# Transposing normalised tokens: TensorE against VectorE squares and a trip through DRAM

## The chip, the cores and the metric

The kernel runs on one core of a Trainium2 chip. A core has TensorE (PE, with its weight loads shown as PEld), VectorE (DVE), ScalarE (ACT), GpSimd (POOL), and the queue engine SyncE (SP), which here only issues DMAs. The metric is device time in microseconds of one execution; the number that counts is the median of several runs.

## The reference

The model is one sandwich layer on x of shape 16 x 256 x 256 (sequences, tokens, width E = 256), all in float32:

```
x = x + layernorm(attention(layernorm(x)))
x = x + layernorm(ffn(layernorm(x)))
```

Attention has 16 heads of 128: q = x Wq^T; shared keys and values kp, vp of width 128, each multiplied per head by a factor kh, vh that comes from a gated, decayed running sum over tokens (weights Wkvh, Wg); rotary embedding on q and k; causal softmax; output through Wout. The FFN has 1024 hidden units with ternary-quantised weights: silu(gate) * up, an RMS norm, and a projection back to 256.

Both products after a layernorm (the projections of attention, and gate and up of the FFN) contract over E. The normalised tokens come with tokens on partitions, and TensorE needs E on partitions, so each normalised sequence (256 x 256) has to be transposed. This transposition is what the change is about.

## The kernel before

The 16 sequences go in 8 pairs (`BP = 2`, a pair has 512 tokens). Each pair has 16 heads, so there are 128 heads in a row, and the main loop has one *slot* for each: `slot(g)` scores head g, softmaxes it, turns the probabilities of head g-1, and forms the output of head g-2. In front of that it prepares the queries of head g+1 and the keys of head g+2. Slot numbers are given below modulo 16, so that "slot 0" is the first head of a pair; the slot is then the same one in each pair.

The order of the instructions on each engine is the order in which the program writes them (`manual_schedule`); no planner moves them. Everything that isn't a head's own work is put into named places of slots: `put(slot, place, step)` appends a step to a plan, and `slot(g)` runs the places in the order first, scored, turned, emptied, projection, last as its own work goes by (in the code below, `fill(g, place)`; the place names come in this order: "first" at the slot's start, "scored" after the next queries' matmuls, "turned" after `queries_done`, then `reciprocals`, "projection", `outputs` of head g-2, "emptied", "last"). Each engine runs its own instructions in order and waits by semaphores for the others.

A slot's own work, by engine:

- PE: scores `sps` (L575), queries `qps` (L285), whatever projection `att` (L735) is planned, head output `ops` (L691, L698).
- DVE: `prob` (L588: mask, scale, row minimum), the head's turn `sq` (L634), the rotary embedding of the next head's queries (L307 twice, L315, and L318, which writes `qT`), and the reciprocals `total` (L609). The next slot's `sps` needs `qT`.
- ACT: `even` (L627: probabilities divided and laid out for the turn), `prob` (L598: exponentials), the copy `oT` (L706).
- POOL: `kT` (L563) and `vph` (L675).
- SP: fetches the key factors `kh` (L545, for four heads ahead), writes the turned probabilities to DRAM (`moved`, L641) and reads them back (`pT`, four reads, L647).

That turn of probabilities (`Head.turn`) already works as the change does: VectorE transposes each 32 x 32 square in place, and the DMAs move the squares to where they belong by way of DRAM. `even` of 128 x 768 takes one DVE instruction, one write and four reads.

The normalised tokens go another way. In `Pair.plan` (attention, pair bp, planned during the pair before) and `After.plan` (FFN, sequence q) a sequence goes through these steps:

- `moments`: DVE statistics (L232 twice, L234 twice);
- `normalise`: POOL takes the inverse root and applies mean and scale, xn (L219, L221, L261; DVE for the first pair);
- `transpose`: four TensorE transposes of 128 x 128 into a PSUM tile (`transposed`, L278, tp_a or tp_f);
- attention: `keep`, an ACT copy into `xnT` (L349). From `xnT` come `hg` (`factors`, gates and head factors), `kp` (`keys`), `vps` (`values`), and all `qps` of the pair;
- FFN: `split` into a high and a low float32r part, `xhi` on ACT (L780) and `xlo` on DVE (L781), from which `gates` and `ups` are multiplied.

For pairs 2 to 7 the attention steps stand in slots 14 to 1 (`s = end - H - 2`, so moments in 14 and 15, transposes in 0 and 1), `hg` in slot 2 "last" and the rotary embedding of the shared keys in slot 5 (`rope.sine` "scored", `keys_done` "emptied"). The FFN of the even sequence of the pair before has its statistics in slot 6 and its transposes and split in slot 8; the odd one has its statistics in slot 0 and transposes and split in slot 2. All of PE's results in the ordinary path go through four PSUM tiles (`ps_mm`, tag "mm"), and the tokens through two buffers `xn`, the turned probabilities through two buffers `sq32`.

Of the kernel before, what the change touches and what calls it, by code (L numbers as in the profile page):

```python
# [9 lines left out]
F32 = mybir.dt.float32  # L10
# [6 lines left out]
P = 128  # L17
B, N, E = 16, 256, 256
# [5 lines left out]
BP = 2  # L24
T = BP * N
NT = T // P
EC = E // P
# [13 lines left out]
def sandwich_kernel(  # L41
# [13 lines left out]
    nc = tc.nc  # L55
# [3 lines left out]
    p2 = ctx.enter_context(tc.tile_pool(name="p2", bufs=2))  # L59
    p3 = ctx.enter_context(tc.tile_pool(name="p3", bufs=3))  # L60
    heads = ctx.enter_context(tc.tile_pool(name="heads", bufs=10))
    dram = ctx.enter_context(tc.tile_pool(name="dram", bufs=2, space=bass.MemoryType.DRAM))
# [36 lines left out]
    for half in range(2):  # L99
        cols = slice(half * H * D // 2, (half + 1) * H * D // 2)  # L100
        nc.scalar.dma_start(
            out=wq_sb[:, :, cols], in_=wq[:, cols].rearrange("(c p) f -> p c f", p=P)
# [120 lines left out]
    class Rows:  # L223
# [35 lines left out]
        def apply(self, dst, src, engine):  # L259
            for t in range(self.count):  # L260
# [6 lines left out]
                    ALU.mult,  # L267
                )

    def tiles(ap):  # L270
        return [ap[:, t, :] for t in range(2)]

    def transposed(xn, name):

        tp = mm_tile([P, EC, N], f"tp_{name}")
        for c in range(EC):
            for t in range(2):
                nc.tensor.transpose(  # L278
                    tp[:, c, t * P : (t + 1) * P], xn[:, t, c * P : (c + 1) * P], ident
                )  # L280
        return tp
# [42 lines left out]
    def put(slot, place, *steps):  # L324
        assert place in PLACES
        plan.setdefault((slot, place), []).extend(steps)


    class Pair:
# [12 lines left out]

        def transpose(self, b):
            self.tp[b] = transposed(self.xn[b], f"a{self.bp}_{b}")

        def keep(self, b):
            if b == 0:
# [144 lines left out]
        def plan(self):  # L492

            end = self.bp * H
            s = end - H - (2 if self.bp > 1 else -1)
            for b in range(BP):
                put(s + b, "scored", lambda b=b: self.moments(b))
                put(s + b, "emptied", lambda b=b: self.normalise(b))
                put(s + 2 + b, "turned", lambda b=b: self.transpose(b))
                put(s + 2 + b, "emptied", lambda b=b: self.keep(b))  # L500
            put(s + 4, "last", self.factors)
            put(s + 5, "first", self.gates)
            put(s + 5, "scored", self.raw_factors)
            put(s + 5, "last", self.keys)
            put(s + 7, "scored", lambda: self.rope.sine(0), lambda: self.rope.sine(1))
            put(s + 7, "emptied", self.keys_done)
            chain = end - (7 if self.bp > 1 else 8)
            put(chain - 2, "emptied", self.sigmoids)
            put(chain - 1, "emptied", self.decays)
            put(chain, "scored", self.decayed)  # L510
            put(chain + 1, "scored", self.sums)
            put(chain + 2, "first", self.rows_out)
            put(chain + 3, "last", self.value_factors)
            put(chain + 4, "first", self.value_factors_done)
            put(end - 1, "last", self.values)
            put(end, "first", self.values_done)
# [194 lines left out]
    class After:  # L711
# [60 lines left out]
        def transpose(self):  # L772
            self.tp = transposed(self.xn, f"f{self.q}")

        def split(self):
            self.parts = [
                self.buffer([P, EC, N], F32R, f"x{k}", f"x{k}", p2)
                for k in ("hi", "lo")
            ]
            nc.scalar.copy(self.parts[0], self.tp)  # L780
            nc.vector.tensor_sub(self.parts[1], self.tp, self.parts[0].bitcast(F32))  # L781
# [224 lines left out]

        def plan(self, s):

            put(s, "scored", self.moments)
            put(s, "emptied", self.normalise)  # L1010
            put(s + 2, "turned", self.transpose)
            put(s + 2, "emptied", self.split)
            if self.late:
                return
            for u in range(FC // 2):
                at = s + 3 + (u + 1) // 2
                put(at, "last" if u % 2 == 0 else "scored", lambda u=u: self.gates(u))
                done = (at + 1, "first") if u % 2 == 0 else (at, "turned")
                put(*done, lambda u=u: self.gates_done(u))
            put(s + 6, "scored", self.silu)  # L1020
            for u in range(FC // 2):
                put(s + 7 + u, "first", lambda u=u: self.hidden(u))
                put(s + 7 + u, "scored", lambda u=u: self.pieces(u))
                put(s + 7 + u, "emptied", lambda u=u: self.square(u))
                put(s + 8 + u, "last", lambda u=u: self.project(u))
            for u in range(FC // 2):
                put(s + 6 + u, "last", lambda u=u: self.ups(u))
            put(s + 12, "first", self.last_moments)
            put(s + 11, "scored", self.fold)
            put(s + 12, "turned", self.sums)  # L1030
            put(s + 12, "emptied", self.sums_done)
            put(s + 13, "scored", self.inverse_roots, self.last_factors)
            put(s + 14, "first", self.finish)
            put(s + 14, "scored", self.store)
# [53 lines left out]
    for pair in all_pairs[1:]:  # L1088
        pair.plan()
        for b in range(BP):  # L1090
            q = pair.bp * BP + b
# [263 lines left out]
```

## Time and profile before

| | us |
|---|---|
| runs: median (lowest to highest of 3) | 1117.67 (1114.88 to 1118.01) |
| the profiled execution, its own time | 1118.2 |
| its span, first to last instruction | 1116.4 |
| one pair, from one slot 13 to the next (633.39 to 764.03) | 130.64 |

In the trace each slot begins with PE's first `sps`. The pair that the prediction reads has these starts (us): slot 0 at 526.10, 1 at 535.29, 2 at 542.75, 3 at 551.61, 4 at 558.72, 5 at 565.47, 6 at 575.33, 7 at 582.46, 8 at 589.58, 9 at 598.00. The pairs 2 to 6 repeat this to a few hundredths of a microsecond but for some slots. Slots 115 and 117, which the prediction speaks of as well, are slots 3 and 5 of the last pair and begin at 940.25 and 954.61.

How to read the lines. The line with the engines' busy times gives busy us, share of the span, and the number of records. In the table by stretches, each row has the stretch, its length, then for PE, PEld, DVE, ACT and POOL the busy us and the records, the granted TensorE clock (1.00 is full), the busy share of the DMA engines, and GB/s. A wait line has the waiting engine and instruction, what it waited for, and total us, times, and the longest. A timeline line has start and duration in us, engine, source line, operation, output<-inputs, shapes and count, and in brackets the idle time of the engine just before it and what ended that. Matmuls overlap and their ends are modelled, so the distance from one start to the next says what an operation holds PE for. SPq lines are the DMA issues.

### The profile page before, as it was taken

Reading aid. Unit: us, or ns where it says so; the run is one execution under the profiler, and the core shown is the slowest. Engines: PE = TensorE matmul, PEld = TensorE weight load, DVE = VectorE, ACT = ScalarE, POOL = GpSimd, SP = SyncE. Lnnn points to the kernel's source line nnn. Section 1 sums busy time; section 2 is a strip of 40 time slices with the busy share of each in tenths; the row PEclk is TensorE's granted clock in tenths of the full one; section 3 lists DMA queues with packets and bytes.
Section 4 is the critical chain, followed back from the end, with each engine's and each line's share of the span. In section 5 each row is a group of like instructions: output and inputs, shape, how many; then the busy total and the mean of one; then the engine's idle time right before and its main releaser. Section 6 shows DMA issues by size and latency. Waiting matters only on the chain.

```text
span 1116.4 us, 18641 instructions
## 1 busy us (share of the span) xinstructions
PE 1073.3 (96%) x5738; PEld 862.4 (77%) x5738; DVE 845.7 (76%) x2303; ACT 740.8 (66%) x2152; POOL 684.1 (61%) x757
## 2 busy tenths in 40 slices
PE   8899998999999999999999999999999999999986
PEld 5577775788778787888778887788878887788786
DVE  5878889867796777968788677877779677776365
ACT  2778766675676757767576766857567675767563
POOL 3767796438656585548665586555855465656343
PEclk9999999999999999999999999999999999999997
DMA  4512224444444444445454454444444444443101
GB/s 151 163 48 69 76 81 152 152 144 141 141 133 126 147 136 141 134 126 157 126 146 131 125 153 135 146 125 152 139 136 138 126 136 137 139 126 109 39 1 38
DMA packets 108611, 137.35 MB, mean 123 GB/s; under 512 B 12192, under 2 KB 76192, under 8 KB 108512
## 3 DMA queue, kind: packets, MB, share of 16 engines
q1 hardware_dynamic: 103344, 125.09, 36.7%
q0 software_dynamic: 2000, 6.56, 1.8%
q10 hardware_dynamic: 3168, 4.52, 1.2%
q8 instruction: 46, 0.75, 0.3%
q14 instruction: 53, 0.43, 0.1%
HBM read 88.41 MB, written 47.71 MB: 122 GB/s over the span
## 4 chain that ended last, share of the span: by engine, by line
PE 73%; DVE 14%; POOL 5%; ACT 5%; issue 2%; DMA 1%; SPq 0%; ACTq 0%; POOLq 0%; DVEq 0%
PE att L735 16%; PE qps L285 14%; PE sps L575 11%; PE ops L691 8%; PE ffn L882 6%; PE ups L789 5%; PE ops L698 4%; PE gps L789 3%; DVE turned_q L307 3%; ACT even L627 2%; DVE sq L634 2%; DVE qps L315 1%; DVE qT L318 1%; PE hg L285 1%; PE vps L285 1%
## 5 line engine op out<-in xcount | busy, mean ns | idle before, releaser
L598 ACT ACTIVATE prob<-prob,low 128x128 f32<-128x128 f32 (+1 forms) x512 | 225.8, 443 | 38.0 <-DVE low L588 37.6
L285 PE MATMUL qps<-xnT,wq_sb 128*128 128x512 f32 x512 | 240.8, 593 | 0.1
L735 PE MATMUL att<-wout_sb,oT 128*128 128x256 f32 x1024 | 239.1, 380 | 0.7 <-ACT oT L706 0.7
L735 PEld LDWEIGHTS att<-wout_sb,oT 128*128 128x128 f32 x1024 | 189.5, 190 | 40.5 <-issue 16.5
L706 ACT COPY oT<-ops 128x512 f32<-128x512 f32 x128 | 74.9, 585 | 217.8 <-PE ops L698 217.6
L588 DVE CUSTOM_DVE_ANT_0 prob<-sps,mask 128x128 f32<-128x128 f32 (+1 forms) x512 | 157.7, 352 | 79.2 <-PE sps L575 78.3
L575 PE MATMUL sps<-kT,qT 128*128 128x128 f32 (+1 forms) x1024 | 193.4, 332 | 18.3 <-DVE qT L318 10.7
L307 DVE TENSOR_TENSOR turned_q<-qps,sin_sb 64x512 f32<-64x512 f32 x256 | 176.2, 688 | 16.7 <-PE qps L285 11.4
L675 POOL TENSOR_TENSOR vph<-vp,vh 128x512 f32<-128x512 f32 x110 | 115.8, 1053 | 99.6 <-PE ops L698 99.6
L575 PEld LDWEIGHTS sps<-kT,qT 128*128 128x128 f32 x1024 | 145.8, 191 | 38.8 <-DVE qT L318 14.3
L563 POOL TENSOR_TENSOR kT<-kh,kr 128x512 f32<-128x512 f32 x128 | 165.6, 1294 | 11.7 <-PE sps L575 9.3
L627 ACT ACTIVATE even<-prob,total 128x128 f32<-128x128 f32 (+1 forms) x440 | 163.9, 446 | 6.6 <-DVE total L609 6.4
L285 PEld LDWEIGHTS qps<-xnT,wq_sb 128*128 128x128 f32 x512 | 95.9, 190 | 67.5 <-issue 61.2
L691 PE MATMUL ops<-pT,vph 128*128 128x256 f32 x440 | 131.4, 380 | 2.5 <-DMA pT<-moved 1.8
L835 POOL TENSOR_TENSOR lo<-h,hi 128x512 fp32r<-128x512 f32 x54 | 68.6, 1271 | 90.6 <-ACT hi L833 90.6
L634 DVE STREAM_TRANSPOSE sq<-even 128x768 f32<-128x768 f32 x110 | 107.2, 974 | 17.5 <-ACT even L627 16.0
L598 ACT ACTIVATION_READ_ACCUMULATOR prob<-prob,low 128x1 f32 x512 | 96.5, 189 | 0.0
L315 DVE TENSOR_TENSOR qps<-qps,cos_sb 128x512 f32<-128x512 f32 x128 | 89.6, 700 | 4.7
L698 PEld LDWEIGHTS ops<-pT,vph 128*128 128x128 f32 x440 | 83.6, 190 | 11.4
L318 DVE TENSOR_TENSOR qT<-qps,turned_q 128x512 f32<-128x512 f32 x128 | 88.6, 692 | 4.4
L853 POOL TENSOR_TENSOR squares<-squares,sq 128x512 f32<-128x512 f32 x39 | 49.9, 1279 | 66.4 <-ACT sq L852 66.4
L691 PEld LDWEIGHTS ops<-pT,vph 128*128 128x128 f32 x440 | 74.4, 191 | 14.9 <-issue 7.2
(165 smaller groups left out, 1950.4 us busy)
## 6 DMA issues: line engine op xcount, KB each, us to landing
moved<-sq SPq DMA_DIRECT2D x110, 384.0 KB, 2.3
pT<-moved SPq DMA_DIRECT2D x440, 96.0 KB, 2.2
kh<-rows SPq DMA_DIRECT2D x126, 256.0 KB, 3.4
xt<-in_x_dram SPq DMA_DIRECT2D x16, 256.0 KB, 2.9
out_dram<-y POOLq DMA_DIRECT2D x13, 256.0 KB, 3.4
wq_sb<-in_wq_dram ACTq DMA_DIRECT2D x2, 1024.0 KB, 9.6
wout_sb<-in_wout_dram ACTq DMA_DIRECT2D x1, 2048.0 KB, 15.6
w_gu<-in_wgu_dram POOLq DMA_DIRECT2D x8, 256.0 KB, 3.4
```

The source lines that it names most:

```text
L285: nc.tensor.matmul(ps, lhs[:, c, :], rhs[:, c, :], start=(c == 0), stop=(c == EC - 1))
L307: self.engine.tensor_mul(by_sequence(self.turned[a : a + HALF, :]), by_sequence(self.src[b : b + HALF, :]), over_sequences(sin_sb[b : b + ...
L563: nc.gpsimd.tensor_mul(self.kT, self.kh, self.pair.kr)
L575: nc.tensor.matmul(sps[:, cols], self.qT[:, n0 + i * P : n0 + (i + 1) * P], self.kT[:, n0 : n0 + (i + 1) * P], start=True, stop=True,)
L588: nc.vector.tensor_tensor_reduce(out=prob[:, cols], in0=sps[:, cols], in1=mask[:, P - i * P :], scale=-SCALE, scalar=F32_MAX, op0=ALU.add, ...
L598: nc.scalar.activation(prob[:, cols], prob[:, cols], AF.Exp, bias=low[:, i : i + 1], scale=-1.0, accum_out=self.total[:, b * 2 + i : b * 2 ...
L627: nc.scalar.activation(dst, src, AF.Copy, scale=self.total[:, 2 * b + i : 2 * b + i + 1])
L634: nc.vector.transpose(turned.rearrange("p k u q -> p (k u q)"), self.even.rearrange("p k u q -> p (k u q)"),)
L675: nc.gpsimd.tensor_mul(self.vp, self.pair.vp, self.pair.vh[:, :, self.h : self.h + 1].to_broadcast([P, NT, D]),)
L691: nc.tensor.matmul(ops[:, n0 : n0 + N], self.vp[:, b * (N // P), :], early, start=True, stop=False,)
L698: nc.tensor.matmul(ops[:, n0 + P : n0 + N], self.vp[:, b * (N // P) + 1, :], late, start=False, stop=True,)
L735: nc.tensor.matmul(self.acc[:, t, :], oT[:, n0 + t * P : n0 + (t + 1) * P], wout_sb[:, h, :], start=(h == 0 and t == 0), stop=(h == H - 1) ...
```

## The change

For attention of pairs 2 to 7 and for the FFN of sequences 2 to 11 the four TensorE transposes of a sequence are gone. In their place `turn_rows` lets VectorE transpose the 32 x 32 squares of the whole sequence in one instruction (128 x 512) and issues one write of 256 KB to DRAM on SP, and `fetch_turned` issues eight reads of 32 KB on SP (four row groups k, two halves c of E). A read takes 32 partitions with eight runs of 32 floats (128 bytes) each. For attention the reads land in `xnT` and the ACT copy falls away. For the FFN they land in a third use of the `xn` buffers, and `split` reads that instead of PSUM. Pairs 0 and 1 and sequences 0, 1 and 12 to 15 keep the transposes on TensorE.

Steps also move. In pairs 2 to 7 `moments` goes from "scored" to "turned", that is on DVE from before the next head's rotary embedding to after it, and so does the sine part of the shared keys. The attention turn stands in slots 15 and 0 ("projection", after the reciprocals), the reads in slots 0 and 1. For the FFN `moments` is in "turned" for all sequences; for 2 to 11 it is earlier, too: for the even one in slot 5, with turn in slot 6, reads in slot 7 and the split in slot 8 as before; for the odd one in slot 10, with turn in 11, reads in 12, and the split in slot 13 in place of slot 2 of the pair after.

```diff
--- before.py
+++ after.py
@@ -267,6 +267,31 @@
                     ALU.mult,
                 )
 
+    def turn_rows(xn, name):
+
+        turned = p2.tile([P, 4, 3 * BP, 32], F32, tag="sq32", name=f"sq32_{name}")
+        turned = turned.rearrange("p k u q -> p (k u q)")[:, : 2 * E]
+        nc.vector.transpose(turned, xn.rearrange("p t e -> p (t e)"))
+        moved = dram.tile(
+            [2 * 4, 32, EC, 4, 32], F32, tag="xmoved", name=f"xmoved_{name}", bufs=3
+        )
+        nc.sync.dma_start(
+            out=moved.rearrange("(t a) j c k i -> (a j) t (c k i)", a=4),
+            in_=turned.rearrange("p (t e) -> p t e", t=2),
+        )
+        return moved
+
+    def fetch_turned(dst, moved, ks):
+        by_square = moved.rearrange("u j c k i -> k c j u i")
+        for k in ks:
+            for c in range(EC):
+                nc.sync.dma_start(
+                    out=dst[32 * k : 32 * k + 32, c, :].rearrange(
+                        "j (u i) -> j u i", i=32
+                    ),
+                    in_=by_square[k, c],
+                )
+
     def tiles(ap):
         return [ap[:, t, :] for t in range(2)]
 
@@ -342,6 +367,14 @@
 
         def transpose(self, b):
             self.tp[b] = transposed(self.xn[b], f"a{self.bp}_{b}")
+
+        def turn(self, b):
+            self.moved = turn_rows(self.xn[b], f"a{self.bp}_{b}")
+
+        def fetch_turned(self, b, ks):
+            if b == 0 and ks[0] == 0:
+                self.xnT = p2.tile([P, EC, T], F32, tag="xnT", name=f"xnT_{self.bp}")
+            fetch_turned(self.xnT[:, :, b * N : (b + 1) * N], self.moved, ks)
 
         def keep(self, b):
             if b == 0:
@@ -493,16 +526,21 @@
 
             end = self.bp * H
             s = end - H - (2 if self.bp > 1 else -1)
+            turned = "turned" if self.bp > 1 else "scored"
             for b in range(BP):
-                put(s + b, "scored", lambda b=b: self.moments(b))
+                put(s + b, turned, lambda b=b: self.moments(b))
                 put(s + b, "emptied", lambda b=b: self.normalise(b))
-                put(s + 2 + b, "turned", lambda b=b: self.transpose(b))
-                put(s + 2 + b, "emptied", lambda b=b: self.keep(b))
+                if self.bp > 1:
+                    put(s + 1 + b, "projection", lambda b=b: self.turn(b))
+                    put(s + 2 + b, "turned", lambda b=b: self.fetch_turned(b, range(4)))
+                else:
+                    put(s + 2 + b, "turned", lambda b=b: self.transpose(b))
+                    put(s + 2 + b, "emptied", lambda b=b: self.keep(b))
             put(s + 4, "last", self.factors)
             put(s + 5, "first", self.gates)
             put(s + 5, "scored", self.raw_factors)
             put(s + 5, "last", self.keys)
-            put(s + 7, "scored", lambda: self.rope.sine(0), lambda: self.rope.sine(1))
+            put(s + 7, turned, lambda: self.rope.sine(0), lambda: self.rope.sine(1))
             put(s + 7, "emptied", self.keys_done)
             chain = end - (7 if self.bp > 1 else 8)
             put(chain - 2, "emptied", self.sigmoids)
@@ -772,6 +810,13 @@
         def transpose(self):
             self.tp = transposed(self.xn, f"f{self.q}")
 
+        def turn(self):
+            self.moved = turn_rows(self.xn, f"f{self.q}")
+
+        def fetch_turned(self):
+            self.tp = p2.tile([P, EC, N], F32, tag="xn", name=f"xfT_{self.q}")
+            fetch_turned(self.tp, self.moved, range(4))
+
         def split(self):
             self.parts = [
                 self.buffer([P, EC, N], F32R, f"x{k}", f"x{k}", p2)
@@ -1006,10 +1051,18 @@
 
         def plan(self, s):
 
-            put(s, "scored", self.moments)
-            put(s, "emptied", self.normalise)
-            put(s + 2, "turned", self.transpose)
-            put(s + 2, "emptied", self.split)
+
+            on_pe = self.q < 2 or self.q > B - 5
+            m = s if on_pe else s - 1 if self.q % BP == 0 else s - 6
+            put(m, "turned", self.moments)
+            put(m, "emptied", self.normalise)
+            if on_pe:
+                put(m + 2, "turned", self.transpose)
+                put(m + 2, "emptied", self.split)
+            else:
+                put(m + 1, "turned", self.turn)
+                put(m + 2, "turned", self.fetch_turned)
+                put(m + 3, ("emptied", "turned")[self.q % BP], self.split)
             if self.late:
                 return
             for u in range(FC // 2):
```

## The prediction

> **What bounds the kernel.** I read the busy shares first, then the same by stretches of 40 us, then TensorE's waits in the five pairs that repeat (250 to 900 us).
>
> ```profile
> PE 1073.3 (96%) x5738; PEld 862.4 (77%) x5738; DVE 845.7 (76%) x2303; ACT 740.8 (66%) x2152; POOL 684.1 (61%) x757
> ```
> ```profile
> 640.00:680.00 40.00, 40.00 (x224) 32.91 (x223) 31.41 (x92) 23.65 (x75) 32.08 (x32) 1.00 0.51 152
> 760.00:800.00 40.00, 40.00 (x223) 32.88 (x222) 29.93 (x88) 26.25 (x78) 29.74 (x35) 1.00 0.46 142
> ```
> ```profile
> PE sps L575 <- DVE qT L318: 4.4, 5, 0.9
> PE sps L575 <- DVE total L609: 1.7, 5, 0.4
> PE ops L691 <- DMA pT<-moved: 0.8, 1, 0.8
> ```
> PE is busy for all 40.00 us of such stretches at a granted clock of 1.00, and waits for 6.9 us in 650. So PE work taken out of these slots is time, unless a wait appears. Only two waits are systematic (five times each, once a pair): 0.9 us at the end of slot 5 (slots are counted modulo 16) and 0.35 at the end of slot 4. Both are for DVE at the end of its rotary embedding; total stands right behind qT there.
>
> What one set of four transposes holds PE for stands in PE's timeline, by starts, since the ends are modelled:
>
> ```profile
> 536.60 1.88 PE L285 MATMUL qps<-xnT,wq_sb 128*128 128x512 f32 x4
> 538.32 0.60 PE L278 MATMUL tp_a<-ident,xn_a 128*128 128x128 f32 x4
> 538.75 1.89 PE L735 MATMUL att<-wout_sb,oT 128*128 128x256 f32 x8
> ```
> 538.32 to 538.75 is 0.43 us; tp_f in the next slot takes 0.47 (546.14 to 546.61). I take 0.44.
>
> **Removed.** The sets of pairs 2 to 7 (12) and of sequences 2 to 11 (10): 22 x 0.44 = **-9.7 us**. Their slots (0 and 1; 2 and 8) have no PE wait now. ACT loses 12 copies xnT (588 ns); it is idle for 2 us and more in slots 0 and 1, so that is worth nothing. The ten splits now read SBUF and not PSUM: by the rows of hi and lo (606 and 757 ns against 584 and 692) 0.02 us on ACT and 0.07 on DVE each, off PE's path: 0.
>
> **DVE: 22 transposes added.** The row for 128x768 is 974 ns, so 128x512 is about 0.65. Each stands after its slot's qT, so it delays the next slot's first DVE work. Slots 1 and 12 start with 3.0 and 2.0 us of DVE idle and slot 0 with about 1: covered. Behind slot 6's transpose the chain is tight:
>
> ```profile
> 582.32 0.17 DVE L609 RECIPROCAL total<-total 128x4 f32<-128x4 f32 x1
> 582.72 0.69 DVE L824 TENSOR_TENSOR h<-ups,h 128x512 f32<-128x512 f32 x1 [0.23 <-PE ups L789]
> ...
> 585.79 1.39 DVE L307 TENSOR_TENSOR turned_q<-qps,sin_sb 64x512 f32<-64x512 f32 x2 [0.18 <-PE qps L285]
> ...
> 587.95 0.69 DVE L318 TENSOR_TENSOR qT<-qps,turned_q 128x512 f32<-128x512 f32 x1
> ...
> 589.38 1.74 DVE L389 RECIPROCAL gate<-gate 64x256 f32<-64x256 f32 x1
> ```
> Slot 7's qT ends at 588.64 and PE wants it at 589.58: 0.94 to spare, less 0.65, plus the idle 0.23 and 0.18. Slot 8's ends at 596.55 for 598.00, and PE comes 0.44 earlier: 1.45 - 0.44 - about 0.6 leaves 0.4. Covered: 0 (bounds 0 to 0.65 x 5 = +3.3, if the cover fails in every pair).
>
> **DVE: moments and key sines moved behind qT.** In slot 5 the sines (1.39) leave qT's path, so the 0.9 us wait there goes. But DVE has no gap from 570.01 (slot 5's transpose, waiting for ACT) to slot 6's qT at 582.41, 0.05 before PE uses it. Sines and the even sequence's moments still come before that qT, in another order: the wait reappears one slot on. I take 0 (bounds -0.9 x 5 to 0). Slots 14 and 15 gain spare time that was not short; slot 14 needs it, for the odd sequence's xlo (0.69) moves from slot 2 to the end of slot 13 and pushes it, and the moments that leave its path (0.94) pay for that.
>
> In two late places a wait does go. The odd split of sequence 11 leaves slot 115:
>
> ```profile
> 941.55 0.69 DVE L781 TENSOR_TENSOR xlo<-tp_f,xhi 128x512 fp32r<-128x512 f32 x1 [2.00 <-ACT xhi L780]
> ```
> ```profile
> 947.18 1.58 PE L575 MATMUL sps<-kT,qT 128*128 128x128 f32 x8 [1.48 <-DVE qT L318]
> ```
> Its end (942.24) holds the first prob, which without it starts 0.9 earlier, and PE waits 1.48 for that slot's qT: **-0.9**. In slot 117 sequence 12's moments (0.94) leave the way of a qT for which PE waits 0.37: **-0.4**; DVE then has 0.93 of idle. Slot 22 has the same order, partly given back: **-0.3**.
>
> **POOL.** Its normalising (3.5 us) is issued 1 to 6 slots earlier or in place. kT and vph behind it are done 5 us or more before use; slot 1 is freed. 0.
>
> **SP and the transfers.** Each set adds a 256 KB write and eight 32 KB reads. SP is in order:
>
> ```profile
> 538.54 0.34 SPq L641 DMA_DIRECT2D moved<-sq  x1
> 540.90 1.75 SPq L647 DMA_DIRECT2D pT<-moved  x4
> 542.74 0.38 SPq L545 DMA_DIRECT2D kh<-rows  x1
> 545.93 0.34 SPq L641 DMA_DIRECT2D moved<-sq  x1
> ```
> The write waits for its DVE transpose; behind it stand only kh (needed three slots on) and the next moved, whose transpose is later on DVE anyway. A pT read issues in 0.44 and lands in 2.2; I give a new one the same: 8 x 0.44 = 3.5 of SP. SP is free from 542.65 to 545.93, so in slot 1 the reads end near 546.2 and, after kh, moved goes out at 546.6 and not 545.93. From there its landing (2.3), three more pT issues (1.3) and pT's landing (2.2) give 552.4; ops(slot 3) stands at 554.7, by three sets less at 553.4: covered by 1.0. After slots 0 and 12, 4.6 us or more are free; after slot 7, 3 us, with slot 8's transpose itself later.
>
> Who waits for the reads: hg in slot 2, which needs both halves of xnT; behind it all of PE's queue stands still. It stands at 549.74, without three sets about 548.4 (b=1 about 0.5 later); the last read is issued at about 545.8 and lands at 548.0. Spare time about 0.9, less in slots where moved lands late (its landing is 1.9 to 4.8): I add **+1.0** for one or two late hg. In pair 2, slot 17's pT issue ends at 160.2 because moved landed 3.9 us after its issue; the reads then land near 166, while hg stands at 164.36: **+1.6**. Extra waits for eight landings each before hg: **+0.3**. The FFN reads: xhi on ACT waits for them, and behind it the next slot's even. They land about 1.5 us before ACT comes to xhi (slot 8: issued by 593.3, landed by 595.5, xhi at 597.3); in slot 13 ACT has 1.8 us of idle behind xhi.
>
> The unknown is 128-byte runs. None is in the trace; the nearest read has 768-byte runs (pT). Lower bound: pT's fastest issue, 302 ns, which gains nothing, since the reads are hidden at 440. Upper bound: its slowest, 1431, for every read: 8 x 1.0 = 8 us more per set. I take the median of pT, whose form (32 partitions, DRAM to SBUF, in several runs each) is nearest.
>
> [...]
>
> **Sum:** -9.7 - 0.9 - 0.4 - 0.3 + 1.0 + 1.6 + 0.3 = -8.4 us. The profiled execution took 1118.2 (span 1116.4), 0.5 above the runs' median 1117.67. So 1109.8 for it, and 1109.3 at the median's level.
>
> **Rivals.**
> A. Reads too slow: *slower*. If a read costs 1.05 us instead of 0.44, a set's reads end 4.9 later; hg is 4.0 late in six pairs (+24), and pT behind gives a little more: -8.4 + 24 = +15.6, 1133. It breaks even at 0.9 + 8.4/6 = 2.3 us later per set, 0.73 us a read. For it: 1.4 us issues exist. Against: the medians are 425 ns, and 256-run reads of xt issue in 0.40 to 0.47.
> B. DVE's cover fails: slots 7 and 8 each lose, up to 3.3, and pT is late in some slots (+1 to 2): 1114.
> C. The slot 5 wait really goes, as ACT or PSUM leave gaps that the new order fills: 5 x 0.9 more: 1105.
> D. Hidden anyway: the 0.44 turn into waits for qT in each slot. Against: qT is 1.35 to 2.8 early in slots 1 to 3. 1118.
>
> **Chances.** Forecast (1106 to 1112) 0.55, B 0.13, C 0.08, D 0.06, A 0.18. The range leaves out C's far end and A's upper part: 1103 to 1122. The bound of a measurable change is 0.3%, 3.4 us: faster takes the forecast, C and half of B (0.69, kept at 0.67); same D and the other half of B (0.13); slower A and a rest (0.20).
>
> **What would show it.** TensorE's transposes fall from 128 records to 40 (tp_a 16, tp_f 24), 22 DVE transposes of 128x512 near 0.65, PE at 40.00 in the middle stretches, a pair's period down from 130.6 to about 128.9 us, the slot 5 wait gone and one like it at slot 6, no DMA wait at hg beyond pair 2. Wrong if hg waits for xnT's reads, ops for pT more than now, or sps for qT at slots 7 and 8.

## The result and the profile after

The changed kernel takes 1147.02 us (median of 6 runs, 1140.40 to 1149.87) against 1117.68 us for the kernel before: a ratio of 1.0254, 95% interval 1.0221 to 1.0286. It is 2.5% slower, where 1109.3 was forecast and 1122 was the range's upper end. The profiled execution took 1142.5, with a span of 1140.7.

The page's busy line and its chain that ended last (the chain of work that leads back from the last instruction), of the changed kernel:

```profile
PE 1073.3 (94%) x5650; PEld 857.1 (75%) x5650; DVE 872.6 (77%) x2325; ACT 737.4 (65%) x2140; POOL 688.4 (60%) x757
...
PE 58%; DVE 17%; ACT 7%; DMA 6%; POOL 6%; issue 4%; SPq 3%; ACTq 0%; POOLq 0%; DVEq 0%
```
The chain of the kernel before:

```profile
PE 73%; DVE 14%; POOL 5%; ACT 5%; issue 2%; DMA 1%; SPq 0%; ACTq 0%; POOLq 0%; DVEq 0%
```
The 88 transposes are gone, yet PE's busy time is the same 1073.3 as before; the last section comes back to that. In the chain SP's issues and the DMAs have 9% together; before they had 1%, and PE 73%. TensorE's waits in the five pairs (250 to 900 us) are no longer VectorE's:

```profile
PE ops L729 <- DMA pT<-moved: 27.5, 12, 3.5
PE ops L729 <- POOL xn_a L261: 1.1, 1, 1.1
PE hg L310 <- DMA xnT<-xmoved_a: 0.7, 1, 0.7
```
The waits for qT and total (4.4 and 1.7 us) have vanished from the list; in their place `ops` waits 27.5 us for the turned probabilities, which in the kernel before cost 0.8. `hg`, which needs the new reads, waits once, 0.7. The prediction had named this as a sign of being wrong ("ops for pT more than now"). So the new transfers are in time, and the old one behind them on the same queue is late. A stretch as the prediction showed it, now with such a wait in it (same columns as there):

```profile
680.00:720.00 40.00, 35.56 (x163) 26.62 (x162) 24.75 (x79) 21.71 (x67) 20.10 (x28) 0.91 0.52 141
```

By slots, start to start of the first `sps`, the pair of the prediction (its slot 0 was at 526.10 before) and two runs of the next section:

| slot | before | after | new order alone | kh behind moved |
|---|---|---|---|---|
| 0 / 1 / 8 | 9.19 / 7.46 / 8.42 | 8.75 / 7.02 / 7.98 | 9.19 / 7.46 / 8.42 | 8.75 / 7.02 / 7.98 |
| 2 | 8.86 | 9.37 | 8.86 | 8.47 |
| 3 | 7.11 | 12.53 | 7.11 | 7.55 |
| 4 / 5 / 6 | 6.75 / 9.86 / 7.13 | 6.24 / 8.81 / 7.07 | 6.75 / 8.81 / 7.47 | 6.30 / 8.82 / 8.33 |
| 9 | 8.94 | 10.27 | 8.94 | 8.94 |
| the pair, from slot 13 to 13 | 130.43 | 136.41 | 129.71 | 128.91 |

The slots that lost a set are 0.44 shorter, to the hundredth. The loss sits in slots 2, 3 and 9, behind the reads. Where it arises is best seen in the first of the five pairs (slots 1, 2 and 3 start at 275.37, 282.39 and 291.39), on SP, of the changed kernel (a timeline line is start, duration, queue, line, operation, output<-input, count):

```profile
272.21 1.75 SPq L685 DMA_DIRECT2D pT<-moved  x4
274.06 3.83 SPq L288 DMA_DIRECT2D xnT<-xmoved_a  x8
277.99 0.40 SPq L278 DMA_DIRECT2D xmoved_a<-sq_a  x1
278.49 0.42 SPq L583 DMA_DIRECT2D kh<-rows  x1
279.00 0.40 SPq L679 DMA_DIRECT2D moved<-sq  x1
283.29 1.74 SPq L685 DMA_DIRECT2D pT<-moved  x4
285.13 3.83 SPq L288 DMA_DIRECT2D xnT<-xmoved_a  x8
289.06 0.39 SPq L583 DMA_DIRECT2D kh<-rows  x1
289.56 0.38 SPq L679 DMA_DIRECT2D moved<-sq  x1
293.64 1.74 SPq L685 DMA_DIRECT2D pT<-moved  x4
295.49 0.38 SPq L583 DMA_DIRECT2D kh<-rows  x1
295.96 0.38 SPq L679 DMA_DIRECT2D moved<-sq  x1
300.14 1.86 SPq L685 DMA_DIRECT2D pT<-moved  x4
```
The turns that these writes wait for, and the `ops` of slot 3 (DVE and PE of the same kernel):

```profile
277.44 0.97 DVE L672 STREAM_TRANSPOSE sq<-even 128x768 f32<-128x768 f32 x1
284.57 0.97 DVE L672 STREAM_TRANSPOSE sq<-even 128x768 f32<-128x768 f32 x1
...
293.81 0.98 DVE L672 STREAM_TRANSPOSE sq<-even 128x768 f32<-128x768 f32 x1 [0.16 <-ACT even L665]
```
```profile
297.35 0.67 PE L729 MATMUL ops<-pT,vph 128*128 128x256 f32 x2 [2.66 <-DMA pT<-moved]
```
Two things are to be seen. First, moved leaves late: the turns end at 278.41, 285.54 and 294.79, the writes go out at 279.00, 289.56 and 295.96, that is 0.6, 4.0 and 1.2 us later, because reads, a write and kh stand in front of them. Second, the distance from moved to the first pT, in front of which SP waits for moved to land (224.9 us in the five pairs, 77 times), is 4.29, 4.08 and 4.18 us; before it was 2.4. Both delays are handed on: a late pT starts the next reads late. The third moved has no reads in front of it and is late all the same.

### The profile page after: what moved, and what is told of

Its sections match the earlier page's. It is cut to its first block, busy times and chain, and to the rows that moved or that the text cites. A ratio compares the mean times of both kernels' runs of the same rounds, so it can differ in the third digit from the quotient of the medians.

```text
span 1140.7 us, 18829 instructions
## 1 busy us (share of the span) xinstructions
PE 1073.3 (94%) x5650; PEld 857.1 (75%) x5650; DVE 872.6 (77%) x2325; ACT 737.4 (65%) x2140; POOL 688.4 (60%) x757
## 4 chain that ended last, share of the span: by engine, by line
PE 58%; DVE 17%; ACT 7%; DMA 6%; POOL 6%; issue 4%; SPq 3%; ACTq 0%; POOLq 0%; DVEq 0%
PE att L773 12%; PE qps L310 11%; PE sps L613 9%; PE ops L729 7%; PE ffn L927 5%; PE ups L834 4%; DVE turned_q L332 3%; PE gps L834 3%; DMA moved<-sq 3%; PE ops L736 3%; DVE sq L672 2%; ACT even L665 2%; DMA pT<-moved 2%; DVE qps L340 2%; DVE qT L343 1%
## 5 line engine op out<-in xcount | busy, mean ns | idle before, releaser
L773 PEld LDWEIGHTS att<-wout_sb,oT 128*128 128x128 f32 x1024 | 190.7, 190 | 48.2 <-issue 23.4
L744 ACT COPY oT<-ops 128x512 f32<-128x512 f32 x128 | 74.9, 585 | 224.9 <-PE ops L736 224.2
L713 POOL TENSOR_TENSOR vph<-vp,vh 128x512 f32<-128x512 f32 x110 | 119.9, 1090 | 82.8 <-PE ops L736 82.8
L729 PE MATMUL ops<-pT,vph 128*128 128x256 f32 x440 | 136.4, 392 | 30.9 <-DMA pT<-moved 28.2
L729 PEld LDWEIGHTS ops<-pT,vph 128*128 128x128 f32 x440 | 74.8, 195 | 48.2 <-issue 41.1
L736 PEld LDWEIGHTS ops<-pT,vph 128*128 128x128 f32 x440 | 85.9, 195 | 12.4
L736 PE MATMUL ops<-pT,vph 128*128 128x128 f32 x440 | 86.6, 279 | 0.0
```

The source lines that it names most:

```text
L713: nc.gpsimd.tensor_mul(self.vp, self.pair.vp, self.pair.vh[:, :, self.h : self.h + 1].to_broadcast([P, NT, D]),)
L729: nc.tensor.matmul(ops[:, n0 : n0 + N], self.vp[:, b * (N // P), :], early, start=True, stop=False,)
L736: nc.tensor.matmul(ops[:, n0 + P : n0 + N], self.vp[:, b * (N // P) + 1, :], late, start=False, stop=True,)
L773: nc.tensor.matmul(self.acc[:, t, :], oT[:, n0 + t * P : n0 + (t + 1) * P], wout_sb[:, h, :], start=(h == 0 and t == 0), stop=(h == H - 1) ...
```

## The experiments

Three theories of the loss, which the expectations call by letters. Q: SP's order; the reads' issues, the new write and kh stand in front of moved, which leaves late. K: kh's 256 KB, now issued just ahead of moved, lengthen its landing. P: the 2,048 packets of 128 bytes that a set adds hold up moved and pT wherever they stand. They don't exclude each other, and each run changes one of them, though some change a second with it, which is then said.

Two quantities are read from SP's timeline in each run: how long after its turn moved is issued, and how long after that the first pT goes out. Means over the five pairs (us, late / distance; the ratio is to runs of the kernel before made beside that run, whose medians are 1116.5 to 1117.7):

| run | slot 1 | slot 2 | slot 3 | slot 8 | median us | ratio to before, 95% |
|---|---|---|---|---|---|---|
| before | 0.0 / 2.6 | 0.0 / 2.5 | 0.0 / 2.4 | 0.0 / 2.8 | 1117.68 | |
| after | 2.0 / 4.5 | 5.6 / 4.3 | 1.2 / 4.2 | 1.8 / 4.3 | 1147.02 | 1.0221 to 1.0286 |
| long runs | 0.9 / 4.3 | 4.2 / 4.1 | 1.4 / 4.2 | 1.3 / 4.1 | 1133.11 | 1.0129 to 1.0163 |
| one read | 0.0 / 3.8 | 0.4 / 3.6 | 0.0 / 2.7 | 0.0 / 2.6 | 1109.68 | 0.9919 to 0.9961 |
| reads behind moved | 0.0 / 4.7 | 0.3 / 4.1 | 0.0 / 2.4 | 0.0 / 2.7 | 1121.71 | 1.0029 to 1.0061 |
| reads on ACT | 0.0 / 2.7 | 0.0 / 2.7 | 0.0 / 2.4 | 0.0 / 2.5 | 1114.98 | 0.9981 to 1.0009 |
| kh behind moved | 0.5 / 3.7 | 2.9 / 2.7 | 0.0 / 2.9 | 0.4 / 2.6 | 1107.76 | 0.9897 to 0.9943 |
| kh behind pT | 1.8 / 3.1 | 4.1 / 2.5 | 0.0 / 3.4 | 1.0 / 2.4 | 1115.23 | 0.9967 to 0.9997 |
| before, kh just ahead | 0.7 / 4.2 | 0.8 / 4.1 | 0.7 / 4.1 | 0.8 / 4.7 | 1137.01 | 1.0144 to 1.0216 |

### The new order without the DMAs

```diff
-                if self.bp > 1:
-                    put(s + 1 + b, "projection", lambda b=b: self.turn(b))
-                    put(s + 2 + b, "turned", lambda b=b: self.fetch_turned(b, range(4)))
-                else:
-                    put(s + 2 + b, "turned", lambda b=b: self.transpose(b))
-                    put(s + 2 + b, "emptied", lambda b=b: self.keep(b))
+                put(s + 2 + b, "turned", lambda b=b: self.transpose(b))
+                put(s + 2 + b, "emptied", lambda b=b: self.keep(b))
...
-            on_pe = self.q < 2 or self.q > B - 5
-            m = s if on_pe else s - 1 if self.q % BP == 0 else s - 6
+            on_pe = True
+            m = s
```


> Edit: TensorE transposes and the ACT copy come back for every sequence, at their old places; only the order of moments and key sines (behind the next head's rotary embedding) stays as in the changed kernel. No write or read of turned tokens is left. Two theories of the loss share one forecast here: the loss comes with the DMAs, so it goes. In the changed kernel slot 4 was 0.5 us shorter than before and slot 5 1.06, five times each: if that is the new order's doing, 7.8 us less than before, about 1110 (1108 to 1113). Rival: those two waits went only because TensorE comes to slots 4 and 5 late, after its new stalls in slots 2 and 3, while VectorE ran ahead; then nothing stays, 1116 to 1119.

Measured: 1115.91 us, ratio 1.0003 (0.9992 to 1.0013). The order of the steps costs nothing in the sum. This run lacks VectorE's 22 new transposes as well as the DMAs, and the FFN's steps are back in their old slots; but several runs below keep the transposes and the moved steps and are without the loss, so it belongs to the DMAs. The rival got the time right and the reason half: the waits of slots 4 to 6 do not simply go. Slot 5 loses 1.05 and slot 6 gains 0.34 in every pair, slot 4 stays. That is worth 3.6 us over five pairs, and pair 2 gives it back: its slots 13 to 28 take 124.04 us against 120.52.

### Packets

```diff
-        by_square = moved.rearrange("u j c k i -> k c j u i")
+        rows = moved.rearrange("u j c k i -> u j (c k i)")
...
-                    out=dst[32 * k : 32 * k + 32, c, :].rearrange(
-                        "j (u i) -> j u i", i=32
-                    ),
-                    in_=by_square[k, c],
+                    out=dst[32 * k : 32 * k + 32, c, :], in_=rows[2 * k + c]
```


> Edit: eight reads of 32 KB in the same places, but each row is read in one run of 1,024 bytes and not eight of 128; the values land in the wrong places, so it leaves out the regrouping of the squares. Issues, bytes and order are those of the changed kernel, packets an eighth. Theory Q: the order is what costs, so the time stays at 1142 to 1150. Theory P: without the small packets moved lands in 2.4 us, the time falls below 1115.

Measured: 1133.11 us, between the two. Eight reads now issue in 3.63 us and not 3.83, and land in 1.7 and not 2.0; the page counts 15,360 packets under 512 bytes and not 60,416. The distance is still 4.1 to 4.3. So small packets cost 13.9 us here, but the larger part of the loss (16.6 of 29 us) stands without them, and it is not they that lengthen moved's landing.

### One issue in place of eight

```diff
-        for k in ks:
-            for c in range(EC):
-                nc.sync.dma_start(
...
+        row = moved.rearrange("u j c k i -> (u j c k i)")
+        nc.sync.dma_start(out=dst, in_=row.rearrange("(p c n) -> p c n", p=P, c=EC))
```


> Edit: each set's eight reads become one of the same 256 KB in runs of 1,024 bytes (values land in the wrong places, so the regrouping of the squares is left out). Against the run with eight reads of long runs (1133.1) only the number of issues differs. Theory Q: SP is held 0.45 and not 3.7 us per set, moved leaves in time or nearly, time 1105 to 1115. If the bytes or the kh in front of moved are what matters: 1125 or more.

Measured: 1109.68 us. With the same bytes and runs, seven issues fewer are worth 23.4 us. moved is in time in slots 1, 3 and 8, and 0.4 late in slot 2; TensorE's waits for pT fall to 1.1 us. SP's time in front of moved starts the loss. The edit changes kh's place in time, too. In the prediction's pair SP is through with kh 2 us before the turn is done, and the distance is 2.5:

```profile
536.35 0.41 SPq L576 DMA_DIRECT2D kh<-rows  x1
538.69 0.33 SPq L672 DMA_DIRECT2D moved<-sq  x1
541.19 1.74 SPq L678 DMA_DIRECT2D pT<-moved  x4
```
In slot 1 of three of the five pairs the distance is still 4.4 to 5.1, and there it costs next to nothing, since moved leaves in time.

### The same reads behind moved

`moving` is a new place of a slot, right behind its moved.

```diff
             nc.sync.dma_start(
                 out=self.moved, in_=turned.rearrange("p k u q -> p k (u q)")
             )
+            fill(g, "moving")
...
-                    put(s + 2 + b, "turned", lambda b=b: self.fetch_turned(b, range(4)))
+                    put(s + 2 + b, "moving", lambda b=b: self.fetch_turned(b, range(2)))
+                    put(s + 3 + b, "moving", lambda b=b: self.fetch_turned(b, range(2, 4)))
...
-                put(m + 2, "turned", self.fetch_turned)
+                put(m + 2, "moving", lambda: self.fetch_turned(range(2)))
+                put(m + 3, "moving", lambda: self.fetch_turned(range(2, 4)))
```


> Edit: the same write and the same eight reads per set on the same queue, but in program order behind a slot's moved write and in front of its pT reads, four in one slot and four in the next, where SP only waits for moved to land (2.4 us; four reads take 1.9). Theory Q (order on SP: reads, write and kh stand in front of moved, which leaves 1 to 7 us late, and the lateness is handed on through pT): moved leaves right behind its transpose again, TensorE's waits for pT fall from 28 us to under 5, time about 1103 (1098 to 1108; the new order of moments gave nothing by itself, so the 9.7 us of transposes are the whole gain). Theory P (2,048 packets of 128 bytes a set hold up moved and pT wherever the reads stand; one-eighth of the packets was worth 14 us): pT waits stay above 15 us, time 1118 or more.

Measured: 1121.71 us. The mechanism is as theory Q has it: moved leaves with its turn, pT waits fall from 27.5 to 0.7 us (the long distances in slots 1 and 2 are now the reads themselves). The time is not: the reads come later, so `hg` waits 2.2 us in two pairs, and the waits for qT are 8.9 us, where the kernel before had 4.4; one is behind slot 9 in every pair, whose `xlo` waits for an `xhi` that now comes later (slot 9 takes 9.53 and not 8.94). Slot 15 is some 0.6 longer, too, which was not followed. One queue was relieved at another consumer's cost.

### The reads on ScalarE's queue

```diff
-                nc.sync.dma_start(
+                nc.scalar.dma_start(
                     out=dst[32 * k : 32 * k + 32, c, :].rearrange(
```


> Edit: the eight reads per set are issued by ScalarE's queue and not by SP's, at the same places of the program. Theory Q: moved leaves at the end of its transpose, pT waits fall under 8 us; ACT pays 8 x 0.45 = 3.6 us per set out of its 34% idle time, and prob and even of the next slot may come some of that late: 1106 to 1122. If packets or bytes are the cause, not the queue: moved on time but landing 4 us later, 1135 or more.

Measured: 1114.98 us, with no pT wait among TensorE's waits of the five pairs. Packets and bytes are unchanged, so it is their place on SP that counts; kh has its lead back here as well (in slots 1 to 3 of the prediction's pair it is issued 1.7 to 3.7 us ahead of moved, and the distances are 2.4 to 2.7 in the mean). ACT pays: over the whole run it idles 30.4 us in front of its copy oT behind the reads of xnT, and 19.4 behind those of the FFN, and TensorE's waits for qT are 9.4 us (slot 8 is 8.94 long and not 7.98).

### kh behind moved

This edit leaves the reads as they are (`turns(head)` is true where a head's probabilities go by way of DRAM, `behind` is the fetch of kh):

```diff
-        if g + 4 < total:
+        if g + 4 < total and not turns(before):
             all_heads[g + 4].fetch()
...
-            before.turn()
+            before.turn(all_heads[g + 4].fetch if g + 4 < total else None)
...
                 out=self.moved, in_=turned.rearrange("p k u q -> p k (u q)")
             )
+            if behind:
+                behind()
```


> Edit: the changed kernel with one thing moved: the fetch of kh for four heads ahead (256 KB) is issued behind a slot's moved write and no longer in front of it. In slots 2 and 3 moved is issued 0.1 us behind kh and pT can go only 4.1 to 5.1 us later, against 2.4 where kh is long gone. Theory K (kh's data just ahead lengthens moved's landing): that distance falls below 3 us in slots 1, 2, 3 and 8, and the time to 1125 to 1138. If it isn't kh: distance 4 us or more, time 1143 to 1150. Theory Q alone (issues) would give 0.5 us per late slot, the kh issue itself, about 1140.

Measured: 1107.76 us, 39 us less than the changed kernel and 0.8% less than before. SP of this run, at the same place as above (slot 2 starts at 282.03):

```profile
278.33 0.41 SPq L679 DMA_DIRECT2D moved<-sq  x1
278.83 0.40 SPq L583 DMA_DIRECT2D kh<-rows  x1
281.26 1.74 SPq L687 DMA_DIRECT2D pT<-moved  x4
283.10 3.83 SPq L288 DMA_DIRECT2D xnT<-xmoved_a  x8
287.03 0.39 SPq L679 DMA_DIRECT2D moved<-sq  x1
287.52 0.38 SPq L583 DMA_DIRECT2D kh<-rows  x1
289.71 1.75 SPq L687 DMA_DIRECT2D pT<-moved  x4
```
The reads still take 3.83 us in front of the second moved, but the distance is 2.93 and 2.68 in place of 4.29 and 4.08, and pT goes out at 289.71 in place of 293.64. TensorE's waits in the five pairs:

```profile
PE sps L613 <- DVE qT L343: 3.9, 5, 1.2
PE ops L731 <- DMA pT<-moved: 2.6, 3, 1.2
```
The distance was expected below 3 us in all four slots; it is 2.6 to 2.9 in slots 2, 3 and 8, and 3.7 in slot 1. Theory K was right in kind and far too small in size (1125 to 1138 expected). That each slot's gain is handed on to the next, as the loss was, would explain the size; this was not measured by itself.

### kh without the change

Two controls on the kernel before. In the first kh goes behind moved there, too (the same edit). In the second it always goes just ahead:

> Edit: the kernel before the change, with only the fetch of kh moved behind moved, as in the run that took the changed kernel to 1107.8. Theory K (kh just ahead of moved lengthens moved's landing): before the change kh is issued 3 us ahead of moved, so there is nothing to gain: 1114 to 1119. If kh's place is worth something by itself, without the reads: 1107 to 1112, and then the gain of the earlier run isn't the change's.

```diff
+            gate = dram.tile([1, 32], F32, tag="gate", name=f"gate_{self.tag}", bufs=3)
+            nc.sync.dma_start(out=gate, in_=turned[0:1, 0, 0, :])
+            if behind:
+                behind()
             nc.sync.dma_start(
                 out=self.moved, in_=turned.rearrange("p k u q -> p k (u q)")
             )
```


> Edit: the kernel before the change, no DMA of tokens, but in every slot SP issues, when the turn is done, a write of 128 bytes that waits for it, then kh, then moved. So kh is always issued right ahead of moved, as the late slots of the changed kernel have it. Theory K: from moved's issue to the first pT 3.8 us or more in every slot, against 2.4 before; with about 0.9 us of two more issues in front, pT comes 2.5 us later everywhere, which eats most of its spare time: 1117 to 1135. If the distance needs the reads (their packets or bytes) and not kh: 2.4 to 2.8, and 1115 to 1119.

Measured: the first 1117.69 us, ratio 1.0005 (0.9991 to 1.0019): nothing to gain, as expected. The second 1137.01 us, and on SP:

```profile
547.96 0.23 SPq L642 DMA_DIRECT2D gate<-sq  x1
548.29 0.34 SPq L545 DMA_DIRECT2D kh<-rows  x1
548.68 0.42 SPq L645 DMA_DIRECT2D moved<-sq  x1
553.00 1.74 SPq L651 DMA_DIRECT2D pT<-moved  x4
```
4.32 us, and 4.15 as the median over the slots of the five pairs, against 2.40 before, with not one read of tokens in the kernel. So it is kh right in front that lengthens moved's landing, by 1.8 us. (The 128-byte write stands in front, too, but the changed kernel has the same distance without it. Whether any other 256 KB would do the same was not tried by itself; in the run with kh behind moved the 256 KB write of turned tokens stands there in slot 1, and the distance is 2.9 in three pairs and 4.8 and 4.9 in the other two.) The time, 2 us above what was expected, has other waits as well (9.8 us for qT), which were not followed.

### kh between pT and the reads

```diff
                 nc.sync.dma_start(
                     out=self.pT[32 * k : 32 * k + 32].rearrange("j a u q -> j a (u q)"),
                     in_=moved[k],
                 )
+            if behind:
+                behind()
```


> Edit: the changed kernel, kh fetched right behind a slot's pT reads, so in slots 0, 1, 7 and 12 the order on SP is pT, kh, eight reads, moved. The kh issue (0.47) still stands in front of moved, but its data have 4 us of lead there. Theory K: moved to first pT at most 3.2 us in slots 1 and 2, time 1108 to 1122. If the run with kh behind moved gained by using SP's idle wait or by the 0.47 alone: distance 4 us or more as in the changed kernel, time 1130 or more.

Measured: 1115.23 us. SP of this run, in slot 2 of the first pair:

```profile
285.19 0.38 SPq L583 DMA_DIRECT2D kh<-rows  x1
285.66 3.83 SPq L288 DMA_DIRECT2D xnT<-xmoved_a  x8
289.59 0.40 SPq L679 DMA_DIRECT2D moved<-sq  x1
292.14 1.73 SPq L685 DMA_DIRECT2D pT<-moved  x4
```
With four microseconds of reads between kh and moved the distance is 3.1 and 2.5 in slots 1 and 2 in the mean, though moved is still 1.8 and 4.1 late. So it is not kh's issue in front of moved that goes with the long distance, but how shortly before moved it stands: 0.5 us ahead, as in the changed kernel, the means are 4.5 and 4.3, and 4.4 us ahead, as in the lines here, 3.1 and 2.5. That much is worth 32 of the 39 us; the other 7 come when kh's issue, too, stands behind moved (1107.8).

### Long runs once more

Both edits shown above together, kh behind moved and the reads in long runs:

> Edit: kh behind moved (1107.8) and the reads in runs of 1,024 bytes (values land in the wrong places, the regrouping is left out). In the changed kernel long runs were worth 14 us. If the packets cost only because they lengthen an SP chain that is already too long, nothing is left to gain here: 1105 to 1108. If the small packets cost something of their own (DMA time that others wait for): 1095 to 1103.

Measured: 1109.31 us against 1107.76 with runs of 128 bytes. The 14 us of the packets existed only inside the chain that was too long.

### Two attempts at a faster kernel

Both start from kh behind moved. The first:

```diff
-            turned = "turned" if self.bp > 1 else "scored"
+            turned = "turned" if self.bp > 2 else "scored"
```


> Edit: kh behind moved (1107.8), and in pair 2 moments and key sines back at their old place (in front of the next head's rotary embedding). All kernels with the new order take 3.0 us more than before in slots 13 to 28, also the one without any DMA of tokens, so it is the order there and not the reads: 1104 to 1106. If it is the reads or the gating of hg by them: 1107 to 1108.5.

Measured: 1107.02 us (1106.18 to 1108.19), the fastest of all, ratio 0.9912 (0.9887 to 0.9936), but not shown to be faster than 1107.76 (1107.25 to 1108.39). In the profiled executions slots 13 to 28 take 120.21 us in place of 123.37, so the 3 us are the order's, though the time lies in the range given for the rival; why the medians show only 0.7 of it stays open. The second, in addition (`moving` here is right behind kh's new place):

```diff
-            m = s if on_pe else s - 1 if self.q % BP == 0 else s - 6
+            m = s if on_pe else s if self.q % BP == 0 else s - 6
...
-                put(m + 2, "turned", self.fetch_turned)
-                put(m + 3, ("emptied", "turned")[self.q % BP], self.split)
+                put(m + 2, ("moving", "turned")[self.q % BP], self.fetch_turned)
+                put(m + 3, ("scored", "turned")[self.q % BP], self.split)
```


> Edit: the last one, and the even FFN sequence's moments back in slot 6, its turn in slot 7, its eight reads behind moved of slot 8 and its split in slot 9. In the kernels where pT isn't late slots 2 to 6 add up to 39.88 us a pair whatever the single slots do, and 39.00 in the run with the new order alone, whose moments stand in slot 6: VectorE's work up to slot 6's qT bounds them. So 0.88 x 5 = 4.4 less: 1100 to 1102. Against: the reads hold pT of slot 8 by 1.5 us and the split may hold slot 9's qT; then 1104 or more.

Measured: 1109.99 us (1107.00 to 1112.28). The gain came (slot 6 is 7.47 and not 8.35 in the prediction's pair) and went again: slot 8 is 0.29 and slot 9 1.07 longer, behind the later split and reads. What is constant from pair to pair, read again, is slots 3 to 6: 31.0 us in each pair with kh behind moved, whether slot 3 takes 7.11 or 8.55.

## Why the prediction was wrong

**Right: what the change takes off.** The term of 0.44 a set, -9.7, holds: slots 0, 1 and 8 are shorter by just that, and with kh behind moved PE's busy time is 1062.9 us, 10.4 less than before. VectorE's cover in slots 7 and 8 held: they take 7.12 and 7.98 there, and nothing waits. The sines did reappear "one slot on": with kh behind moved slot 5 loses 1.04 and slot 6 gains 1.20, and slots 3 to 6 add up to 31.0 against 30.85. The run with the new order alone (30.14) shows why: the sines' move is worth 0.7, and the even FFN sequence's moments, which now stand in slot 5, take it back; with these moments in slot 6 again, the second attempt has 30.14 to 30.62. Slot 115 went from 6.93 to 6.13 (-0.8, predicted -0.9), slot 117 from 9.38 to 8.84 (-0.5, predicted -0.4), slot 22 from 7.13 to 6.90 (-0.2, predicted -0.3). So a kernel as the sum described it exists: 1109.3 was forecast, and 1107.8 is measured once kh is out of the way. That it comes so near is partly luck, as the next paragraph says.

**Wrong in kind: pair 2.** Its slots 13 to 28 cost 2.9 us more (120.52 to 123.38), where 1.6 were put down to late reads. The run without any read shows the same loss (124.04), and the old order removes it (120.21). The three terms for late reads, 2.9 together, were met by this loss of 2.9, which has another cause.

**Right: the reads.** Issue 0.48 apart, landing 2.0; `hg` waited once for 0.7, against +1.0 in the sum. The +0.3 there for eight landings comes from no row, and no run shows it; that one wait of 0.7 is all that `hg` has in the five pairs. Rival A had the sign and the nearest number, 1133, from a mechanism that did not occur. (Of the xt reads that spoke against it, one of sixteen took 1.44 to issue, not 0.40 to 0.47.) Copies of squares that VectorE has turned were to be seen in the kernel before, too: its pT reads are such copies, and they landed in 2.2.

**Wrong: the step "SP and the transfers", "covered by 1.0".** It put the wait of `ops` for pT at nothing; it measured 27.5 us in the five pairs. The step holds four errors, in the order in which they work.

1. "After slots 0 and 12, 4.6 us or more are free". From the end of slot 0's pT (273.96) to the end of slot 1's turn (278.41) there were 4.45 us, and SP needed 5.04 up to moved (279.00): eight reads, the other sequence's write and kh. The write had been named but its 0.5 us were not added, a read takes 0.48 and not 0.44, and slot 0 itself is 0.44 shorter. Nor was "or more" read rightly: after slot 0, three of the five pairs before the change have 4.6, one 3.9 and one 2.6, where slot 0's moved landed later. moved was 0.6 late here and 2.0 in the mean, where 0 was taken.
2. "From there its landing (2.3)". The row was true for a moved issued 3 us behind kh. The reads took that lead away: the distance is 4.2 to 4.5 us in the mean of each of the four slots. This error weighs most: kh behind moved brings 39 us, kh with 4 us of lead 32, and kh just ahead (with 0.7 us of issues in front of moved) costs some 20 us even without a read, 1137.0 against 1117.4. But the loss of 29 needs the late issues, too: with one read in place of eight it is gone although some distances stay as long.
3. Each slot was worked out as if it began in step. But SP waits for moved, then issues pT, then the reads, then kh, then the next moved. One turn of that loop takes 4.2 + 1.74 + 3.92 + 0.5 = 10.4 us in a slot with reads and 6.5 without (in the lines above 10.56 and 6.40, from one moved to the next), while slots 1 and 3 are 7.0 and 7.1 long. Before, it took 2.4 + 1.74 + 0.1 + 0.4 = 4.6. So lateness grows over two slots with reads (0.6 to 4.0) and is still there in the third, which has none.
4. moved in slot 2 was put 0.7 late; it was 4.0 late here and 5.6 in the mean.

The sixteen reads of slots 0 and 1 had all been counted; what failed was taking a landing time from a row whose neighbour in the queue was about to change.

The turn by way of VectorE and DRAM is 2.5% slower than TensorE's as the change was written and 0.8% faster when kh goes behind moved. Reads in runs of 128 bytes land in 2.0 us and reads in runs of 1,024 in 1.7, and in the whole the short runs cost 14 us or nothing, depending on the chain around them.

## What to carry to other kernels

When transfers are added to a queue that issues in program order, as SP did here, write its whole round down in that order, landing times included, and compare it with the shortest slots in a row (here 10.4 us against 7.0 and 7.1), not with the free time of one slot. Ask of each urgent write what will then stand just ahead of it: a large fetch that nobody needs for three slots belongs behind it, and here moving that one fetch was worth 39 us. One read in place of eight was worth nearly as much, 37 us (its squares are not regrouped). And when a run comes out badly, first read which old transfer is late, before blaming the new one.

## What the runs showed of the hardware that I had not expected

Some stalls cost more than their length here. After some of the waits for pT the granted TensorE clock falls; two stretches of the changed kernel (columns as in the prediction), the wait at 565.31 to 569.31 and the 4 us behind it:

```profile
565.31:569.31 4.00, 0.45 (x3) 0.03 (x1) 3.89 (x8) 2.02 (x8) 0.00 (x0) 1.00 0.49 128
569.31:573.31 4.00, 4.00 (x17) 3.64 (x18) 1.99 (x9) 0.59 (x1) 2.58 (x5) 0.57 0.51 139
```
At that clock the first matmuls of `ops` take up to 1.19 us in place of 0.67, and slot 3 grows by 5.4 us for a wait of 3.55. Of the changed kernel's pT waits over 2 us in the five pairs, five are followed by 4 us at 0.57 to 0.66 (waits of 2.06, 2.38, 2.96, 3.09 and 3.55) and four are not (2.02, 2.16, 2.29 and 2.66); none below 2 us is, nor any of the six waits of 0.8 to 0.9 in the kernel before. In each of the five the clock is 0.50 for 3.41 us, from 422.58, 569.36, 695.65, 705.89 and 842.42 us on, that is from 0.61 us before the wait's end (at 423.19) to 1.31 behind it (at 841.11). The 3.41 us before the drop at 705.89, where the wait of 2.06 us ends, and the drop:

```profile
702.48:705.89 3.41, 1.36 (x4) 0.31 (x3) 3.17 (x6) 2.93 (x12) 0.19 (x1) 1.00 0.63 163
705.89:709.30 3.41, 3.40 (x12) 3.04 (x13) 3.38 (x13) 0.47 (x1) 0.57 (x3) 0.50 0.43 145
```
PE was idle for 2.05 to 3.36 us of the 3.41 us before each of the five drops. In the 3.41 us up to the end of the four other waits it was idle for 2.02 to 2.66 us, and the 4 us behind them have a clock of 1.00. What sets a wait of 2.06 us with a drop apart from one of 2.66 without is not shown. Five times 3.41 x 0.5 is 8.5 us, by this estimate about what the missing transposes should have taken off PE's busy time (9.7 in the prediction).

The first read of a 384 KB write goes 2.4 us after the write's issue in the kernel before; with a 256 KB fetch (kh, one row of DRAM spread over 128 partitions) issued just ahead of the write it is 4.15, and in the changed kernel with the same fetch just behind it 2.6 (medians of the five pairs). In the run on ScalarE's queue, 32 us shorter than the changed kernel, kh has its lead back as well, so how much of the gain is issue time is not shown; the reads land there in 2.6 to 2.7 us and not in 2.0.
